# Opening attention behind the last chunk step: the last batch's ending as pieces inside attention's first steps

## The chip, the core and the metric

The kernel runs on one core of a Trainium2 chip. The metric is the device time of one launch in microseconds (us). The time before is the median of three runs; the profile is of one further execution. Five engines appear in it: TensorE (PE, with its weight loads as PEld), VectorE (DVE), ScalarE (ACT), GpSimd (POOL) and SyncE (SP, which here only issues transfers). ACT and POOL issue transfers as well.

## The reference

The program is two layers on 8 batches of 512 tokens with 256 features. The first adds a state-space block and a top-1 mixture of experts to the input; the second adds an attention block and a capacity-limited top-2 mixture.

```python
x  = u                                            # (8, 512, 256) f32
xn = layernorm(x)
x  = x + ssd_block(xn) + ffn_top1(xn)             # layer 0
xn = layernorm(x)
x  = x + attention(xn) + ffn_top2(xn)             # layer 1

def ssd_block(u):       # chunked scan of 128 tokens, forward and backward
    z, xBC, dt = split(u @ in_proj.T)
    ...
    yg = y * silu(z)                                            # "gate"
    yn = yg * rsqrt(mean(yg * yg, -1) + 1e-5) * norm_w          # "squares", "scale"
    return yn @ out_proj.T                                      # "output"

def attention(x):       # 16 heads of 16
    q = x @ Wq;  latent = (x @ Wk + x @ Wv) @ W_down
    k = latent @ W_up_k;  v = latent @ W_up_v
    s = clip(q k^T / 16) * decay(|i - j|);  a = softmax(clip(s))
    return (a @ v) @ Wo

def ffn_top2(x):        # 7 experts and one that does nothing, 512 rows of capacity each
    w = softmax(x @ router.T + b);  keep the two largest
    each expert takes the first 512 tokens that chose it, in order
    return sum of weight * relu(rows @ W1[e]) @ W2[e], and x * weight for the idle expert
```

## The kernel before

The instructions of each engine stand in the order in which the program traces them (`tc.manual_schedule`), so the order of generators and `yield`s in the source is the order on the chip. An engine's instruction waits only for semaphores of what it reads, or of what last used the place that it writes.

**Layer 0.** The scan runs in 64 chunk steps, 8 for each batch. A step issues a chunk's own work and some pieces of its neighbours (`others(n)`): the next batch's convolutions, and the past batch's ending: `gate` (reads the tokens `u` by a transfer, multiplies y by z, squares), `squares` (the matmul `ss`, L1040, and its copy), `scale` (the matmul `sm`, L1047, and a reciprocal root), and `output` (the matmul `op`, L1060, for each of four token tiles, and `xr`, L1067, the addition of the tokens). Between them `fill(k)` advances two other generators: `rows`, the layer-0 experts, and when these are at an end `rest`, which is `late()`.

**The chain `late()`.** It first loads the weights of layer 1 (`second_weights`, in which `base`, L860, is computed) and then turns three generators in rotation: `norm(b)` (layer norm of batch b, stored as `xn1`), `turn(b)` (two transposed halves `tp1`, L737; the router's `pp1`, L744, copied to `proj1` by DVE, L749; then `project`: `lp` L246 and its copy `lat`, `qp` L261 twice, `kp` L270 twice, `vp` L279 twice, each copied by ACT and stored to DRAM) and `route(lo, hi)` (which expert slots the tokens take: DVE and POOL work, the matmuls `both`, L172, and one accumulated matmul group `tab1` (L226) for each batch, built from DVE's `en_r`, `en_w` and added to `slots`, L819). `route` runs for batches 0 to 4, and then for 5 to 7, which needs `pp1` of batch 7.

**Banks.** Every one of these matmul groups takes a PSUM buffer by `bank(...)` and gives it back when ACT or DVE has copied it. In layer 0 the endings take the tag "gen" and `late()` the tag "e", each with two buffers. In attention `bank` is this:

```python
def bank(name, shape):
    return psum.tile(shape, FP, name=name, tag="bank", bufs=1)
late_bank = bank
```

so that `late()`, the experts and `finish` share one buffer there. Of the other seven, scores (`s_ps`) have four, transposes (`p_ps`) two and values (`o_ps`) one.

**The end of layer 0.** After chunk step 63 the ending of batch 7 runs as a block of its own, with `fill` between its pieces, and only then do the pools of layer 0 close and those of attention open, at the same places.

**Attention.** There are 128 steps (batch b, group g of four heads, token tile c). Step n issues the scores (L1533: four matmuls), the clamp and the banded row maximum on DVE (L1538, L1540), then for older steps the exponentials on ACT (L1548), four transposes of 128x512 (L1555) with their copies on ACT (L1556), and, every second step, the values (L1564). Between these pieces `fill()` advances one thing: `urgent` work first, the experts as far as `due()` allows, and else `late()` through `last_rows(1)`. When `late()` is at an end, the pools of its tiles close and the experts of layer 1 start (`e_tp` L1375, `e_hp` L1383, `e_yp` L1396); `due()` spreads them evenly up to step 117. `spread` (L1418) loads q and k of a batch by groups of 16 rows: 16 transfers each. For batch 0, q goes by SP and k by ACT, traced ahead of the first step. `divide`, `finish` and `combine` normalise, project and add up the results.

**Pools.** A tile's place is freed when its pool closes. What takes a place in a pool opened later waits for the old occupants of it.

Of the kernel before, what the change touches and what calls it, by code (L numbers as in the profile page):

```python
# [17 lines left out]
P = 128  # L18
# [41 lines left out]
def tile_kernel(ctx: ExitStack, tc: tile.TileContext, t, out: bass.AP):  # L60
# [237 lines left out]

    l0 = ctx.enter_context(ExitStack())
    l0c = l0.enter_context(tc.tile_pool(name="l0c", bufs=1))  # L300
    m1 = l0.enter_context(tc.tile_pool(name="m1", bufs=1))
    m2 = l0.enter_context(tc.tile_pool(name="m2", bufs=2))
    mp = l0.enter_context(tc.tile_pool(name="mp", bufs=1, space=PSUM))
    r0 = ExitStack()
    r0p = r0.enter_context(tc.tile_pool(name="r0", bufs=2))
    r0b = r0.enter_context(tc.tile_pool(name="r0b", bufs=1))
# [5 lines left out]
    def ask():  # L312
        pool, tag, bufs = ((m1, "z", 1), (m2, "yT", 2), (m2, "yT", 2), (m2, "bc", 2))[len(us)]
        both = pool.tile([P, HC, S], FP, name=tag, tag=tag, bufs=bufs).rearrange("p k s -> p (k s)")
        us.append(both.rearrange("p (t d) -> p t d", d=DM))
        for k in range(2):
            Y.dma_start(
                out=us[-1][:, k * TPB : (k + 1) * TPB, :], in_=rows_of(t["u"], order[2 * len(us) - 2 + k])
            )
# [14 lines left out]
    w_out = ctile("w_out", [P, HC, DM], pool=l0c)  # L334
# [5 lines left out]
    share = ctile("share", [P, 1], pool=l0c)  # L340
# [223 lines left out]
    with ExitStack() as es:  # L564
# [28 lines left out]
        def blocks():  # L593
            nonlocal e2
            r0.close()
            e2 = es.enter_context(tc.tile_pool(name="e2", bufs=2, side="right"))
# [74 lines left out]
        def late():  # L671
# [12 lines left out]
            def norm(b):  # L684
# [4 lines left out]
                if b == B - 1:  # L689
                    x = final  # L690
                else:
                    if b not in asked:
                        ask(b)
                        yield
                        yield
                        add(b)
                        yield
                        yield
                        yield
                    x = asked.pop(b)  # L700
                    Y.dma_start(out=rows_of(x1, b), in_=x)
# [27 lines left out]
            def turn(b):  # L729
# [18 lines left out]
                yield  # L748
# [12 lines left out]
            def route(lo, hi):  # L761
# [5 lines left out]
                with tc.tile_pool(name=f"rt{lo}", bufs=1, side="right") as pool:  # L767
# [33 lines left out]
                with tc.tile_pool(name=f"en{lo}", bufs=1, side="right") as pool:  # L801
# [31 lines left out]
        def second_weights():  # L833
# [3 lines left out]
            l1c = ctx.enter_context(tc.tile_pool(name="l1c", bufs=1, side="right"))  # L837
            tl = tls.enter_context(tc.tile_pool(name="tl", bufs=1, side="right"))
# [65 lines left out]
        class Batch:  # L904
# [68 lines left out]
            def start(self):  # L973

                self.yT = p2.tile([P, HC, S], FP, name="yT", tag="yT")

                def first(k):
                    by = V if self.b else G
                    by.tensor_tensor(self.yT[:, k, :], self.x[:, k, :], self.fr[k], ALU.mult)
                    if k + 2 < HC:  # L980
                        self.ask(k + 2)

                def second(k):
                    y, x = self.yT[:, k, :], self.x[:, k, :]
                    for to, of in ((slice(1, S), slice(0, S - 1)), (slice(0, S - 1), slice(1, S))):
                        V.scalar_tensor_tensor(y[:, to], x[:, of], d_rep[:, k : k + 1], y[:, to], ALU.mult, ALU.add)

                return chain([(p, k) for k in range(HC) for p in (first, second)])
# [25 lines left out]
            def z_part(self, o):  # L1014

                if o == 0:
                    self.z = p1.tile([P, HC, S], FP, name="z", tag="z")
# [5 lines left out]
            def gate(self):  # L1023
                self.u = p1.tile([P, TPB, DM], FP, name="u", tag="u", bufs=2)
# [32 lines left out]
            def output(self, c):  # L1057
# [6 lines left out]
                def add():  # L1064
# [3 lines left out]
                    if c == TPB - 1:  # L1068
                        Y.dma_start(out=rows_of(x1, self.b), in_=final if self.b == B - 1 else self.u)
# [125 lines left out]
        with tc.manual_schedule(engines=ENGINES):  # L1195
# [116 lines left out]
            pending.append(last.gate())  # L1312
            while pending:
                slot()
                fill(1)
            last.squares()
            fill(3)
            slot(last.scale)
            fill(3)
            slot()  # L1320
            while B - 4 not in turned:
                fill(1)
            final = tl.tile([P, TPB, DM], FP, name="xr", tag="xr", bufs=3)
            for c in range(TPB):
                slot(lambda: last.output(c))
                fill(2)
            slot()
            batch_done = B
    l0.close()
# [3 lines left out]
    res = l1.enter_context(tc.tile_pool(name="res", bufs=1))  # L1333
    x_sb = res.tile([P, NTILE, DM], FP, name="x_sb", tag="x_sb")
    with tc.tile_pool(name="a1", bufs=1) as p1, tc.tile_pool(name="a2", bufs=2) as p2, tc.tile_pool(
        name="ap", bufs=1, space=PSUM
    ) as psum, ExitStack() as es:

        def bank(name, shape):
            return psum.tile(shape, FP, name=name, tag="bank", bufs=1)  # L1340
# [69 lines left out]
        def spread(rows, got, n, by=None):  # L1410

            for g in range(4):
                wide = p2.tile([P, S], FP, name=n + "T", tag=n + "T", bufs=6)
# [16 lines left out]
        def inputs_of(b):  # L1430
            rows, vd = kept.pop(b)
            got = {"q": [], "k": [], "v": p2.tile([P, TPB, VW], FP, name="vt", tag="vt")}
# [29 lines left out]
        class Ending:  # L1462
# [22 lines left out]
            def project(self):  # L1485
# [3 lines left out]
                V.tensor_tensor(x_sb[:, self.i, :], x_sb[:, self.i, :], fp, ALU.add)  # L1489
                Y.dma_start(out=out[self.i * P : (self.i + 1) * P, :], in_=x_sb[:, self.i, :])  # L1490

        def finish(b, oT):
            for c in range(TPB):
# [3 lines left out]
                fo = p2.tile([P, DM], FP, name="fo", tag="fo")  # L1497
                A.copy(fo, fp)
                xi = x_sb[:, b * TPB + c, :]
# [4 lines left out]
        def combine():  # L1504


            def add(b):
                G.dma_start(out=x_sb[:, b * TPB : (b + 1) * TPB, :], in_=rows_of(x1, b), accum_op=ALU.add)
# [7 lines left out]
            for b in range(B - 1):  # L1516
                G.dma_start(out=rows_of(out, b), in_=x_sb[:, b * TPB : (b + 1) * TPB, :])
# [3 lines left out]
        class Step:  # L1521
# [4 lines left out]
            def scores(self):  # L1526
# [7 lines left out]
                self.p = [p2.tile([P, S], FP, name="s1", tag="s1", bufs=12) for _ in range(4)]  # L1534
                mx = p2.tile([P, 4], FP, name="mx", tag="mx", bufs=4)
                self.ng = p2.tile([P, 4], FP, name="ng", tag="ng", bufs=4)
# [13 lines left out]
            def transpose(self, pT, heads):  # L1550
                cc = self.c % 2
                for i in heads:
                    pp = psum.tile([P, TPB, P], FP, name="p_ps", tag="p_ps", bufs=2)
# [16 lines left out]
        def divide(b, g, op, od, rd, held):  # L1570


            if b == B - 1:
                if g == 0:
                    held.append(p1.tile([P, KC, S], FP, name="oT", tag="oT"))
# [12 lines left out]
            if j == 0:  # L1588
                held.append(p1.tile([P, KC, S], FP, name="oT", tag="oT"))
# [20 lines left out]
        with tc.manual_schedule(engines=ENGINES):  # L1610
            rows, vd = kept.pop(0)
            got = {"q": [], "k": [], "v": p2.tile([P, TPB, VW], FP, name="vt", tag="vt")}
            spread(rows["q"], got["q"], "q", Y)
            spread(rows["k"], got["k"], "k", A)
# [17 lines left out]
            def last_rows(k):  # L1632

                nonlocal late_left
                for _ in range(k):
                    if next(rest, "end") == "end":
                        late_left = False
# [22 lines left out]
            def follow():  # L1660
# [4 lines left out]
                elif ready is None:  # L1665
                    ready = n
                    tls.close()
                    e1 = es.enter_context(tc.tile_pool(name="f1", bufs=1, side="right"))
                    e2 = es.enter_context(tc.tile_pool(name="f2", bufs=2, side="right"))
# [5 lines left out]
            def own_rows(b):  # L1675
                Y.dma_start(out=x_sb[:, b * TPB : (b + 1) * TPB, :], in_=rows_of(xn1, b))
# [6 lines left out]
            for n in range(N + 3):  # L1683

                if n < N:
# [7 lines left out]
                    if b == B - 1 and g == 0:  # L1693
                        xi = x_sb[:, b * TPB + c, :]
# [19 lines left out]
                begun = n >= 1  # L1714
                m = n - 2
                pair = m >= 2 and m % 2 == 0
                if pair:

                    s = done[m - 1]
                    if s.c == 1:  # L1720
                        s_op = psum.tile([P, S], FP, name="o_ps", tag="o_ps", bufs=1)
# [8 lines left out]
                if 0 <= m < N:  # L1730
                    if m % 2 == 0:
                        s_pT = [p2.tile([P, TPB, 2 * P], FP, name="pT", tag="pT", bufs=5) for _ in range(4)]
# [108 lines left out]
```

## Time and profile before

| | |
|---|---|
| median of three runs | 2022.19 us (2018.9, 2033.09, 2022.19) |
| the profiled execution | 2011.26 us |
| its span | 2009.5 us |
| PE busy | 1818.5 us, 90% |
| DVE busy | 1459.0 us, 73% |
| ACT busy | 1176.2 us, 59% |
| POOL busy | 587.2 us, 29% |
| mean granted TensorE clock | 0.943 |

The page gives the busy time of each engine, and the span cut into 40 slices of 50.2 us, each with a digit for the busy tenths. "PEclk" is the clock that TensorE was granted, as a share of full speed. In lists of instructions, `out<-in` names the tiles by the program's names, an L number is a line of the kernel, and square brackets hold the idle time before a group with what ended it. Times within the span count from its start. The profiled execution is 10.9 us shorter than the median of the runs.

### The profile page before, as it was taken

Reading aid. Unit: us, or ns where it says so; the run is one execution under the profiler, and the core shown is the slowest. Engines: PE = TensorE matmul, PEld = TensorE weight load, DVE = VectorE, ACT = ScalarE, POOL = GpSimd, SP = SyncE. Lnnn points to the kernel's source line nnn. Section 1 sums busy time; section 2 is a strip of 40 time slices with the busy share of each in tenths; the row PEclk is TensorE's granted clock in tenths of the full one; section 3 lists DMA queues with packets and bytes.
Section 4 is the critical chain, followed back from the end, with each engine's and each line's share of the span. In section 5 each row is a group of like instructions: output and inputs, shape, how many; then the busy total and the mean of one; then the engine's idle time right before and its main releaser. Section 6 shows DMA issues by size and latency. Waiting matters only on the chain.

```text
span 2009.5 us, 33675 instructions
## 1 busy us (share of the span) xinstructions
PE 1818.5 (90%) x11956; PEld 1239.9 (62%) x11956; DVE 1459.0 (73%) x3344; ACT 1176.2 (59%) x2575; POOL 587.2 (29%) x528
## 2 busy tenths in 40 slices
PE   6566999899999999998898869999999999999997
PEld 6224677676767767664565546666666666666654
DVE  6587675767667576778557477878888878788885
ACT  4232454434545454454552337878887887788886
POOL 0042665655556574543330000101011111111030
PEclk8677999999999999998898679999999999999999
DMA  7010565545556554436553313222313222223171
GB/s 267 6 47 26 211 212 171 180 143 172 197 171 206 170 189 160 161 104 172 154 165 93 98 44 108 66 84 57 89 49 103 66 85 54 87 57 100 40 143 42
DMA packets 132967, 238.58 MB, mean 119 GB/s; under 512 B 20381, under 2 KB 94111, under 8 KB 120896
## 3 DMA queue, kind: packets, MB, share of 16 engines
q1 hardware_dynamic: 101952, 119.99, 19.1%
q0 software_dynamic: 29808, 115.78, 18.7%
q8 instruction: 96, 1.57, 0.3%
q10 hardware_dynamic: 1040, 0.66, 0.1%
q14 instruction: 71, 0.58, 0.1%
HBM read 183.58 MB, written 53.71 MB: 118 GB/s over the span
## 4 chain that ended last, share of the span: by engine, by line
PE 66%; DVE 14%; ACT 11%; issue 2%; DMA 1%; POOL 0%; SPq 0%; ACTq 0%; DVEq 0%; POOLq 0%
PE p_ps L1555 8%; PE h_ps L634 6%; PE pj L915 6%; PE y_ps L655 6%; ACT s L1548 6%; PE o_ps L1564 6%; PE s_ps L1533 4%; PE e_hp L1383 4%; PE e_yp L1396 4%; ACT pT L1556 3%; PE op L1060 3%; PE yd L1141 3%; PE seg L1103 2%; PE sp L1171 2%; PE yoff L1159 2%
## 5 line engine op out<-in xcount | busy, mean ns | idle before, releaser
L1538 DVE TENSOR_SCALAR s<-s_ps 128x512 f32<-128x512 f32 x512 | 318.0, 684 | 137.2 <-PE s_ps L1533 135.5
L1548 ACT ACTIVATE s<-s,ng 128x512 f32<-128x512 f32 x512 | 330.9, 717 | 10.9 <-DVE ng L1544 10.9
L1540 DVE CUSTOM_DVE_ANT_0 s<-s,band 128x512 f32<-128x512 f32 x512 | 323.1, 689 | 0.0
L1556 ACT COPY pT<-p_ps 128x512 f32<-128x512 f32 x512 | 276.0, 588 | 65.1 <-PE p_ps L1555 57.1
L1555 PE MATMUL p_ps<-ident,s 128*128 128x128 f32 x2048 | 285.7, 283 | 21.1 <-ACT pT L1556 15.0
L1555 PEld LDWEIGHTS p_ps<-ident,s 128*128 128x128 f32 x2048 | 236.1, 144 | 95.5 <-ACT pT L1556 31.7
L1403 POOL DMA_INDIRECT x<-e_yo,number x28 | 45.9, 1639 | 626.8 <-ACT e_yo L1402 620.8
L915 PE MATMUL pj<-xT,w_w_in 128*128 128x512 f32 x384 | 201.1, 650 | 12.7 <-DVE cv L928 6.6
L634 PEld LDWEIGHTS h_ps<-xdT,w 128*128 128x128 f32 x1248 | 151.7, 195 | 20.6 <-issue 19.8
L1533 PE MATMUL s_ps<-kT,qT 16*128 16x512 f32 x1024 | 157.4, 659 | 5.3 <-DMA kT<-kd 2.2
L928 DVE SCALAR_TENSOR_TENSOR cv<-pj,w_conv_w,cv 128x511 f32<-128x511 f32 (+2 forms) x192 | 143.3, 747 | 22.7 <-ACT cv L924 18.2
L634 PE MATMUL h_ps<-xdT,w 128*128 128x128 f32 x1248 | 155.0, 279 | 0.1
L655 PE MATMUL y_ps<-w,hT 128*128 128x256 f32 x624 | 147.7, 380 | 0.0
L1087 POOL TENSOR_TENSOR au<-da,half 128x512 f32<-128x512 f32 x64 | 78.4, 1225 | 202.8 <-PE seg L1103 131.7
L655 PEld LDWEIGHTS y_ps<-w,hT 128*128 128x128 f32 x624 | 115.7, 190 | 32.4 <-issue 17.1
L1383 PE MATMUL e_hp<-e_xdT,e_w 128*128 128x256 f32 x448 | 121.5, 394 | 10.9 <-ACT e_hT L1386 8.8
L915 PEld LDWEIGHTS pj<-xT,w_w_in 128*128 128x128 f32 x384 | 71.1, 203 | 96.0 <-issue 81.1
L1564 PE MATMUL o_ps<-pT,vt 128*32 128x256 f32 x2048 | 126.8, 386 | 0.0
L1150 DVE TENSOR_TENSOR yT<-yT,yd 128x512 f32<-128x512 f32 (+1 forms) x64 | 43.8, 684 | 98.8 <-PE yd L1141 98.3
L1396 PE MATMUL e_yp<-e_w,e_hT 128*128 128x256 f32 x448 | 113.3, 385 | 0.2 <-ACT e_hT L1386 0.2
L1564 PEld LDWEIGHTS o_ps<-pT,vt 128*32 128x32 f32 x2048 | 61.1, 111 | 83.0 <-issue 49.6
L1116 ACT ACTIVATE mt<-seg,mid 64x64 f32<-64x64 f32 x512 | 109.4, 309 | 0.7
(326 smaller groups left out, 3033.4 us busy)
## 6 DMA issues: line engine op xcount, KB each, us to landing
ex<-exd SPq DMA_DIRECT2D x96, 128.0 KB
fr<-fdd SPq DMA_DIRECT2D x64, 128.0 KB
od<-os SPq DMA_DIRECT2D x28, 256.0 KB
e_w<-in_ei_dram SPq DMA_DIRECT2D x7, 1024.0 KB
e_w<-in_eo_dram SPq DMA_DIRECT2D x7, 1024.0 KB
vd<-vt SPq DMA_DIRECT2D x16, 288.0 KB
vt<-vd SPq DMA_DIRECT2D x8, 576.0 KB
u<-in_u_dram SPq DMA_DIRECT2D x8, 512.0 KB
```

The lines of the kernel that those rows point to most:

```text
L634: T.matmul(hp[:, i, :], w1[:, k * FF + f * P : k * FF + (f + 1) * P], xdT[:, k * P : (k + 1) * P], start=(k == 0), stop=(k == KC - 1),)
L655: T.matmul(yp, hT[f // 4][:, f % 4, :], w2[:, f * DM : (f + 1) * DM], start=(f == 0), stop=(f == FC - 1))
L915: T.matmul(pj, w_in[:, k, o * P : (o + 1) * P], self.xT[:, k, :], start=(k == 0), stop=(k == KC - 1))
L1383: T.matmul(hp, w1[:, k, f * P : (f + 1) * P], xdT[:, k, :], start=(k == 0), stop=(k == KC - 1))
L1396: T.matmul(yp, hT[:, f, c * P : (c + 1) * P], w2[:, f, :], start=(f == 0), stop=(f == FC - 1))
L1533: T.matmul(sp[i], self.q[r, cols], self.k[r, :], start=True, stop=True)
L1538: V.tensor_scalar(self.p[i], sp[i], -CLAMP, CLAMP, ALU.max, ALU.min)
L1540: V.tensor_tensor_reduce(out=self.p[i], in0=self.p[i], in1=band[:, at : at + S], scale=1.0, scalar=-3.0e38, op0=ALU.mult, op1=ALU.max, acc ...
L1548: A.activation(self.p[i], self.p[i], AF.Exp, bias=self.ng[:, i : i + 1])
L1555: T.transpose(pp[:, k, :], self.p[i][:, k * P : (k + 1) * P], ident)
L1556: A.copy(pT[i][:, :, cc * P : (cc + 1) * P], pp)
L1564: T.matmul(op[32 * i : 32 * i + 32, half * 2 * P : (half + 1) * 2 * P], self.v[:, k, h * (AD + 1) : h * (AD + 1) + 32], pT[i][:, k, :], st ...
```

## The change

It has three parts, and the order of the instructions up to chunk step 63 is the same.

First, the block after chunk step 63 becomes a generator `ending()`. Only work that is already pending is drained before the pools close. `last_rows(1)`, called by `fill()` in attention, now advances `end_chain` and `rest` by one piece each, and `fill()` works from step 0 on (`begun = True`) where it worked from step 1 on.

Second, tiles that the ending needs (`z`, odd batches' `yT` and `u`, `w_out`, `share`) lie in a pool `mz` that stays open into attention. The sums `x_sb` are cut into four pieces, two of which take the places of `yT` and `z` in `mz` later, and `oT` takes that of `u`. Attention's one two-buffer pool and its PSUM pool are cut into several pools by tag, with the same numbers of buffers except `fo`, which has six where it had two.

Third, nearly all pools are opened with `reuse_waits="tile"`: a tile at a used place waits for the tiles that lay there, where it waited before for all that the older pool held there.

Besides, the store of `x1` for the last batch is issued by `norm`, k is loaded ahead of q for batch 0, and `turn` has one `yield` fewer in the last two batches.

```diff
+    mz = ctx.enter_context(tc.tile_pool(name="mz", bufs=1, reuse_waits="tile"))
     l0 = ctx.enter_context(ExitStack())
-    l0c = l0.enter_context(tc.tile_pool(name="l0c", bufs=1))
+    l0c = l0.enter_context(tc.tile_pool(name="l0c", bufs=1, reuse_waits="tile"))
...
-    w_out = ctile("w_out", [P, HC, DM], pool=l0c)
+    w_out = ctile("w_out", [P, HC, DM], pool=mz)
...
                     x = asked.pop(b)
-                    Y.dma_start(out=rows_of(x1, b), in_=x)
+                Y.dma_start(out=rows_of(x1, b), in_=x)
...
-                yield
+                if b < B - 2:
+                    yield
                 V.tensor_copy(proj1[:, b * TPB : (b + 1) * TPB, :], pp)
...
-                self.yT = p2.tile([P, HC, S], FP, name="yT", tag="yT")
+                pool, tag = (mz, "yTz") if self.b % 2 else (p2, "yT")
+                self.yT = pool.tile([P, HC, S], FP, name="yT", tag=tag, bufs=1)
...
-                self.u = p1.tile([P, TPB, DM], FP, name="u", tag="u", bufs=2)
+                pool, tag = (mz, "uz") if self.b % 2 else (p1, "u")
+                self.u = pool.tile([P, TPB, DM], FP, name="u", tag=tag)
...
-                    if c == TPB - 1:
-                        Y.dma_start(out=rows_of(x1, self.b), in_=final if self.b == B - 1 else self.u)
+                    if c == TPB - 1 and self.b < B - 1:
+                        Y.dma_start(out=rows_of(x1, self.b), in_=self.u)
...
             last = batch[B - 1]
-            pending.append(last.gate())
             while pending:
                 slot()
-                fill(1)
+            gated = last.gate()
+
+        def ending():
+            nonlocal gated, final, batch_done
+            while callable(gated):
+                gated = gated()
+                yield
+            yield
             last.squares()
-            fill(3)
-            slot(last.scale)
-            fill(3)
-            slot()
+            yield
+            last.scale()()
+            yield
             while B - 4 not in turned:
-                fill(1)
+                yield
             final = tl.tile([P, TPB, DM], FP, name="xr", tag="xr", bufs=3)
             for c in range(TPB):
-                slot(lambda: last.output(c))
-                fill(2)
-            slot()
+                last.output(c)()
+                yield
             batch_done = B
+
+        end_chain = ending()
     l0.close()
...
-    x_sb = res.tile([P, NTILE, DM], FP, name="x_sb", tag="x_sb")
-    with tc.tile_pool(name="a1", bufs=1) as p1, tc.tile_pool(name="a2", bufs=2) as p2, tc.tile_pool(
-        name="ap", bufs=1, space=PSUM
-    ) as psum, ExitStack() as es:
+    sums = {}
+
+    def x_of(b):
+        two = b // 2
+        if two not in sums:
+            pool, tag = (res, "x0") if two == 0 else (res, "x1") if two == 1 else (mz, "yTz") if two == 2 else (mz, "z")
+            both = pool.tile([P, HC, S], FP, name="x_sb", tag=tag, bufs=1).rearrange("p k s -> p (k s)")
+            sums[two] = both.rearrange("p (t d) -> p t d", d=DM)
+        return sums[two][:, b % 2 * TPB : (b % 2 + 1) * TPB, :]
+
+    with ExitStack() as es:
+
+        def pool(name, bufs=1, **kw):
+            return es.enter_context(tc.tile_pool(name=name, bufs=bufs, reuse_waits="tile", **kw))
+
+        p1, pk, p2, pq = pool("a1"), pool("ak"), pool("a2", 2), pool("aq")
+        few, turns, psum = pool("ab", space=PSUM), pool("at", space=PSUM), pool("ap", space=PSUM)
 
         def bank(name, shape):
-            return psum.tile(shape, FP, name=name, tag="bank", bufs=1)
+            return few.tile(shape, FP, name=name, tag="bank", bufs=1)
...
-                fo = p2.tile([P, DM], FP, name="fo", tag="fo")
+                fo = p2.tile([P, DM], FP, name="fo", tag="fo", bufs=6)
...
+            spread(rows["k"], got["k"], "k", A)
             spread(rows["q"], got["q"], "q", Y)
-            spread(rows["k"], got["k"], "k", A)
...
                 for _ in range(k):
-                    if next(rest, "end") == "end":
-                        late_left = False
+                    late_left = [next(one, "end") for one in (end_chain, rest)] != ["end", "end"]
...
-                begun = n >= 1
+                begun = True
```

## The prediction

> **What bounds the kernel now.** First the page's forty slices (50.2 us each), for where TensorE is idle or slow. PE is busy for nine tenths through most of the second half, but in slices 22 and 23 (1105 to 1206 us) the digits fall to 8 and 6, and the granted clock to 0.6 and 0.7. That is where attention opens, and where the diff works.
>
> ```profile
> PE   6566999899999999998898869999999999999997
> ...
> PEclk8677999999999999998898679999999999999999
> ```
>
> Then the busy times of four stretches, cut where the work changes: from the scores of the last chunk step to the first scores of attention (1128.70), to the first transpose of batch 7 (1146.60, "point A"), to the first expert transpose (1224.60), and on to 1900. The columns are PE, PE weight loads, DVE, ACT, POOL, then PE's granted clock and the DMA share. The fifth row is a part of the first stretch.
>
> ```profile
> 1074.00:1128.70 54.70, 48.52 (x241) 35.30 (x239) 27.10 (x87) 13.19 (x24) 1.43 (x2) 0.81 0.23 66
> 1128.70:1146.60 17.90, 13.07 (x33) 6.03 (x33) 12.92 (x41) 1.99 (x4) 0.00 (x0) 0.50 0.48 148
> 1146.60:1224.60 78.00, 57.95 (x364) 37.74 (x364) 54.08 (x170) 38.69 (x69) 4.38 (x5) 0.74 0.24 77
> 1224.60:1900.00 675.40, 645.41 (x5181) 437.50 (x5178) 552.80 (x1410) 555.50 (x1036) 70.28 (x50) 1.00 0.26 72
> 1098.00:1112.00 14.00, 13.33 (x47) 11.09 (x47) 3.99 (x19) 2.34 (x4) 0.00 (x0) 0.51 0.12 43
> ```
>
> Once the experts run, PE is busy 645.41 of 675.40 us (96%): it is the bound. In the 150.6 us before that it is busy 48.52 + 13.07 + 57.95 = 119.5 us, 79%, and DVE 94.1. So some 31 us of PE idleness lie there, partly at half clock. The chain of waits says why attention opens at 1128.7: the last addition of `output` releases the loads of kT and qT, because the new pools lie where the old ones were.
>
> ```profile
> 1125.44 0.49 DVE xr L1067
> 1125.94 0.02 issue
> 1125.96 2.33 DMA kT<-kd
> 1128.29 0.02 issue
> 1128.31 4.03 DMA qT<-qd
> ```
>
> The PE timeline gives the pace of the `bank` fills on either side.
>
> ```profile
> 1077.33 1.72 PE L246 MATMUL lp<-xT,w_kv 128*64 128x256 f32 x8
> 1081.12 3.63 PE L261 MATMUL qp<-xT,w_w_q 128*128 128x512 f32 x4 [2.07 <-DVE proj L749]
> ...
> 1100.74 3.66 PE L226 MATMUL tab<-en_w,en_r 128*128 128x56 f32 x16 [0.67 <-ACT vt L280]
> ...
> 1125.33 1.14 PE L279 MATMUL vp<-w_uv,lat 64*128 64x256 f32 x8
> ...
> 1146.60 1.95 PE L737 MATMUL tp<-ident,xr 128*128 128x128 f32 x4 [1.77 <-ACT xr L721]
> ...
> 1161.75 1.97 PE L246 MATMUL lp<-xT,w_kv 128*64 128x256 f32 x8 [5.44 <-DVE proj L749]
> ...
> 1171.14 1.13 PE L270 MATMUL kp<-lat,w_uk 64*128 64x256 f32 x4 [0.69 <-ACT qc L263]
> ...
> 1179.29 1.13 PE L279 MATMUL vp<-w_uv,lat 64*128 64x256 f32 x4
> ```
>
> From the `lp` at 1077.33 to the end of the last `vp` at 1126.47 there are 28 fills of a bank (lp, qp, tab, qp, tab, ss, and so on). There are two tags of two buffers each, so a fill need not wait for the evacuation of the one just before it: 49.1 / 28 = 1.75 us a fill. From 1146.60 to 1180.42, inside attention, the same kinds of fill (two tp, pp, lp, two qp, two kp, two vp) have one buffer: 33.8 / 10 = 3.4 us a fill. The idle of 5.44 us before `lp` is a fill waiting until DVE, busy with a step's rows, copies `proj`.
>
> **The change, part by part.** (1) Attention opens behind chunk step 63. Its loads no longer wait for the place (pools reuse by tile, some tiles live in `mz`). In the compiled order of the changed kernel the first scores stand right behind `pp` of batch 6, so they start near 1080 and not at 1128.7. The 28 fills then follow on the one `bank`, between steps 0 to 3. Nothing of their work is removed: gate, squares, scale, four outputs, batch 6's projections, the five table passes all stay.
>
> (2) What it brings: at the transpose of batch 7 (call it point B) attention has issued the scores of steps 0 to 4, against 0 to 2 at A. From B to the first expert transpose the order is that of before: seven steps lie between, 78 us. So two steps are done earlier and need not be done at the end. A step's PE work is taken from the groups:
>
> ```profile
> L1538 DVE TENSOR_SCALAR s<-s_ps 128x512 f32<-128x512 f32 x512 | 318.0, 684 | 137.2 <-PE s_ps L1533 135.5
> ...
> L1540 DVE CUSTOM_DVE_ANT_0 s<-s,band 128x512 f32<-128x512 f32 x512 | 323.1, 689 | 0.0
> ...
> L1555 PE MATMUL p_ps<-ident,s 128*128 128x128 f32 x2048 | 285.7, 283 | 21.1 <-ACT pT L1556 15.0
> ...
> L1533 PE MATMUL s_ps<-kT,qT 16*128 16x512 f32 x1024 | 157.4, 659 | 5.3 <-DMA kT<-kd 2.2
> ...
> L1564 PE MATMUL o_ps<-pT,vt 128*32 128x256 f32 x2048 | 126.8, 386 | 0.0
> ```
>
> (285.7 + 157.4 + 126.8) / 128 = 4.45 us on PE, and (318.0 + 323.1) / 128 = 5.0 us on DVE. PE bounds the later stretch, so two steps are worth 2 × 4.45 / 0.956 = 9.3 us. The ends are nothing (if the cover only moves idle time) and 13.0 us (two steps at their own pace with experts between them: 77 steps from 1300 to 1800 us, 6.49 us each). I take 9.3.
>
> (3) What it costs: B against A. `lp` in the new order waits for `proj`, which stands on DVE behind the eight row operations of step 0. `pp` ends at 1077.4; scores at half clock 2.3 us (the four at 1128.70), DVE 5.0, the copies round them 1.3 (an estimate from the 0.6 us rows of ACT and DVE): `lp` at about 1086, 9 us later than now. Then 28 fills: at 1.75 us each B is 1086 + 49 = 1135; at 3.4 us each it is 1086 + 95 = 1181. My walk through the order with every wait named (`tab` waits for ACT's `qc`; `qp` and `kp` wait for DVE's `slots`, itself behind `en_r`, `en_w` and the rows of a step) gives 1165 if all matmuls run at the full-clock durations of before, and 1198 if all run at half clock (a `tab` 3.66 us instead of 1.96, a `qp` 3.63 instead of 1.96). I take 1181: the fills are of the same kinds, have the same single buffer and the same step work between them as the ten that were measured, and it lies between the walks. B − A = +34.6 us; by the walks +18.4 and +51.4.
>
> [...]
>
> On the clock, the row from 1098 to 1112 shows 0.51 with PE busy for 13.33 of 14.00 us. [...]
>
> (4) Queues. The sixteen kT issues go to ACT's queue at about 1076, ahead of the gate's squares and of `lat`; from 1125.96 to 1137.45 they took 11.5 us now, 0.72 us each. `lat` is wanted about 1088, when they are through: 0 us, covered by step 0's DVE work and the wait for `proj`; without that cover up to 11.5 us, and `kp` would be late next, with PE waiting for it. The sixteen qT issues go to SP behind the load of `u` (10.9 us); behind them wait vt, `w_o` and later vd stores, none wanted before the first `o_ps`: 0 to 4 us (qT's landing at 1128.31 took 4.03), I take 0. The `x1` store of batch 7 moves from the output to `norm`, one issue of 0.43 us each way: 0. The swap of k before q and two fewer idle turns: 0, within a fill (3.4 at most either way).
>
> (5) Waits by tile elsewhere. At 878.9 DVE stands 2.58 us because `base` takes a place whose pool waits for a DMA. In the new order that wait is gone, and so are some on POOL and SP. Between 0 (other work hides it) and 2.6 us; I take 2, since DVE's row work follows at once. Deeper `fo` buffers: 0, `finish` is 28 pieces spread over the stretch where PE is 96% busy.
>
> **Sum.** +34.6 − 9.3 − 2 = +23 us on the profiled execution's 2011.26: 2034 (its span of 2009.5 becomes 2033). The median shown is 2022.19, 10.9 above that execution, so I carry the difference to it: 2045. The ends of this mechanism: +18.4 − 13.0 − 2.6 = +3 (2025) and +51.4 − 9.3 − 2 = +40 (2062).
>
> **Rivals.** *Faster: the one bank doesn't bind.* While a fill waits, PE now has transposes and scores of a step to do, which it lacked before. If each fill turns round in the 1.75 us of the two-tag stage, B is 1135, 11.6 us ahead of A, and the sum −11.6 − 9.3 − 2 = −23: 1999. For it: PE idles 31 us of 150 there, which steps could fill. Against it: the 3.4 us were measured with steps between the fills. It decides from B = 1157.9 on, that is 2.57 us a fill.
>
> *About no change: the clock stays full.* Step work in the gaps keeps PE busy, B is the 1165 of the full-clock walk, and the sum +18.4 − 9.3 − 2 = +7: 2029. For it: 0.81 in the first stretch, where PE was 89% busy. Against it: 0.50 and 0.74 once attention runs with one buffer.
>
> *Half clock throughout.* +40: 2062. For it the 0.50 from 1128.70 to 1146.60, in which two or three steps and no experts run, as they would from 1080 on; against it 0.74 from 1146.60.
>
> *The change doesn't do what it says.* If the first loads still wait for a place or a DMA until 1126, the scores stand at 1128.7 as now, and the 28 fills behind them: all of the forecast 48.7 us later, +72, 2094. In the compiled order the first kT load waits for one POOL operation of the last chunk and older DMAs only.
>
> **How the numbers follow.** Chances: forecast 0.45, full clock 0.22, half clock 0.15, faster 0.15, not as said 0.03. A measurement of this kernel can tell about 1% from no change: 2002 to 2042. The forecast's own range is 2030 to 2062, and a third of it lies below 2042; with the full-clock case that makes 0.15 + 0.20 + 0.02 of others for the same, 0.16 for faster, 0.47 for slower. The range 2008 to 2068 leaves out most of the faster case and a little at the top.
>
> **What would show it.** Right: first `s_ps` near 1080, `tp` of batch 7 near 1181, the first expert transpose near 1259 behind scores of step 11, a granted clock of 0.5 to 0.8 between, PE waits before fills released by ACT `qc`, `kc`, `vt` and DVE `proj`, `slots`, and from 1259 on the stretch to the end shorter by 9 us. Wrong: `tp` of batch 7 before 1158, or fills that no longer wait for an evacuation, or first scores still near 1128.

## The result and the profile after

The changed kernel takes 2030.41 us (median of 20 runs, 2026.55 to 2040.45) against 2016.80 us (20 runs, 2009.38 to 2033.09): a ratio of 1.0064, 95% interval 1.0047 to 1.0081, so it is slower by 13 us (13.6 between the medians). The profiled execution after took 2028.93 us, its span is 2027.2 us. The forecast was 2045, slower, by 23 us.

The slices of the page after, with 50.7 us each: the dip is longer. The four slices 21 to 24 (1064 to 1267 us) have the digits 6, 7, 7 and 8 and a clock of 0.6, 0.6, 0.8 and 0.7, where before slices 21 to 23 had 8, 8 and 6.

```profile
PE   6557999998999999998896778999999999999997
...
PEclk8678999999999999998896687999999999999999
```

The busy times of stretches after, cut at the same events as before: batch 5's transposes to the first late fill `lp`, on to batch 7's transposes, on to the first expert transpose, and on. Columns: PE, PE weight loads, DVE, ACT, POOL, granted clock, DMA share, GB/s.

```profile
1069.40:1084.49 15.09, 5.24 (x34) 3.60 (x32) 12.62 (x48) 2.41 (x5) 1.44 (x2) 0.69 0.65 141
1084.49:1179.48 94.99, 75.23 (x313) 48.29 (x313) 41.02 (x121) 24.76 (x44) 0.00 (x0) 0.68 0.18 60
1179.48:1252.29 72.81, 57.61 (x377) 37.93 (x373) 51.83 (x167) 36.01 (x65) 4.43 (x5) 0.78 0.21 70
1252.29:1900.00 647.71, 621.40 (x4979) 422.73 (x4976) 527.69 (x1342) 531.21 (x992) 71.29 (x50) 1.00 0.27 75
```

The same events in the PE timeline before: batch 5's transposes, the first scores of attention, the first expert transpose (batch 7's transposes, at 1146.60, stand in the prediction).

```profile
1073.60 1.34 PE L737 MATMUL tp<-ident,xr 128*128 128x128 f32 x8
...
1128.70 2.27 PE L1533 MATMUL s_ps<-kT,qT 16*128 16x512 f32 x4 [2.22 <-DMA kT<-kd]
...
1224.64 0.66 PE L1375 MATMUL e_tp<-ident,e_xd 128*128 128x128 f32 x4
```

The PE timeline after shows the mechanism row by row: the first scores at 1073.61 and not at 1128.70, then `lp` held back behind step 0's rows on DVE, then a fill, a wait for its copy, and the next fill.

```profile
1069.38 1.04 PE L738 MATMUL tp<-ident,xr 128*128 128x128 f32 x8
...
1073.61 2.10 PE L1560 MATMUL s_ps<-kT,qT 16*128 16x512 f32 x8 [0.69 <-DMA kT<-kd]
1084.49 1.97 PE L246 MATMUL lp<-xT,w_kv 128*64 128x256 f32 x8 [8.77 <-DVE proj L751]
...
1097.84 3.66 PE L226 MATMUL tab<-en_w,en_r 128*128 128x56 f32 x16 [0.74 <-ACT qc L263]
1103.12 2.04 PE L270 MATMUL kp<-lat,w_uk 64*128 64x256 f32 x4 [1.61 <-DVE slots L821]
1105.89 3.66 PE L226 MATMUL tab<-en_w,en_r 128*128 128x56 f32 x16 [0.73 <-ACT kc L272]
...
1179.48 1.12 PE L738 MATMUL tp<-ident,xr 128*128 128x128 f32 x4
...
1185.19 1.08 PE L246 MATMUL lp<-xT,w_kv 128*64 128x256 f32 x8 [0.28 <-DVE proj L751]
...
1252.29 0.66 PE L1401 MATMUL e_tp<-ident,e_xd 128*128 128x128 f32 x4
```

And on DVE, between step 0's clamp and the copy of `proj` that `lp` waits for:

```profile
1078.52 2.48 DVE L1565 TENSOR_SCALAR s<-s_ps 128x512 f32<-128x512 f32 x4
...
1084.16 0.18 DVE L751 COPY proj<-pp 128x32 f32<-128x32 f32 x1
```

From `lp` to batch 7's transposes 28 fills took 94.99 us: 3.39 us each. Within them PE stood 95.0 − 75.2 = 20 us, and worked at a mean clock of 0.68. (The `pp` that the prediction calls batch 6's is batch 5's; batch 6's is one of the 28 fills. Nothing in the sum hangs on it.)

Cut at the same three events, batch 5's transposes (T5), batch 7's (T7) and the first expert transpose, the two profiled executions differ like this:

| stretch, us | before | after | difference | predicted |
|---|---|---|---|---|
| start to T5 | 1073.60 | 1069.38 | −4.2 | −2 |
| T5 to T7 | 73.00 | 110.10 | +37.1 | +34.6 |
| T7 to experts | 78.04 | 72.81 | −5.2 | 0 |
| experts to the end | 784.86 | 774.91 | −10.0 | −9.3 |
| span | 2009.5 | 2027.2 | +17.7 | +23 |

The profiled execution of before lies 5.5 us below the median of its 20 runs and that after 1.5 below, which is the 4 us between +17.7 here and +13.6 in the medians. The −4.2 up to T5 lies within the scatter of T5 (below).

### The profile page after: what moved, and what is told of

Read it like the earlier page. It is cut to its first block, busy times and chain, and to the rows that moved or that the text cites. A ratio compares the mean times of both kernels' runs of the same rounds, so it can differ in the third digit from the quotient of the medians.

```text
span 2027.2 us, 33672 instructions
## 1 busy us (share of the span) xinstructions
PE 1824.0 (90%) x11956; PEld 1239.6 (61%) x11956; DVE 1460.0 (72%) x3344; ACT 1175.8 (58%) x2575; POOL 591.7 (29%) x528
## 4 chain that ended last, share of the span: by engine, by line
PE 69%; DVE 15%; ACT 11%; issue 3%; DMA 1%; POOL 0%; SPq 0%; ACTq 0%; DVEq 0%; POOLq 0%
PE p_ps L1582 8%; PE pj L917 7%; PE h_ps L635 6%; PE y_ps L656 6%; PE o_ps L1591 6%; ACT s L1575 5%; PE s_ps L1560 4%; PE e_hp L1409 4%; PE e_yp L1422 4%; ACT pT L1583 3%; PE op L1064 3%; PE yd L1145 3%; PE seg L1107 2%; DVE cv L930 2%; PE sp L1175 2%
## 5 line engine op out<-in xcount | busy, mean ns | idle before, releaser
L1560 PE MATMUL s_ps<-kT,qT 16*128 16x512 f32 x1024 | 151.9, 654 | 0.7 <-DMA kT<-kd 0.7
```

The lines of the kernel that those rows point to most:

```text
L1560: T.matmul(sp[i], self.q[r, cols], self.k[r, :], start=True, stop=True)
```

## The experiments

Theory: the fills are dear since each waits for the copy of the one before it in the single `bank`. Rivals: the half clock would cost the same with any number of buffers; the steps' rows on DVE hold the copies back; the pools and places cost the time. All ratios are against the kernel before, run on the same chip.

The events of each profile, in us:

| kernel | T5 | first scores | T5 to T7 | T7 to experts | experts to end | ratio, 95% interval |
|---|---|---|---|---|---|---|
| before | 1073.6 | 1128.7 | 73.0 | 78.0 | 784.9 | 1 |
| after | 1069.4 | 1073.6 | 110.1 | 72.8 | 774.9 | 1.0064 (1.0047 to 1.0081) |
| two places | 1078.3 | 1081.8 | 78.5 | 74.3 | 772.2 | 0.9918 (0.9897 to 0.9939) |
| four places | 1067.7 | 1071.1 | 82.6 | 73.9 | 772.2 | 0.9884 (0.9860 to 0.9909) |
| four, and scores' place later | 1071.0 | 1074.5 | 78.2 | 68.8 | 772.1 | 0.9884 (0.9858 to 0.9911) |
| four, one piece ahead | 1068.7 | 1077.6 | 76.0 | 81.3 | 772.5 | 0.9912 (0.9879 to 0.9945) |
| after, one piece ahead | 1070.1 | 1081.8 | 114.6 | 81.4 | 772.3 | 1.0104 (1.0075 to 1.0132) |
| after, yield put back | 1072.1 | 1075.9 | 110.6 | 78.5 | 772.4 | 1.0095 (1.0070 to 1.0120) |
| after, ending as a block | 1075.5 | 1134.2 | 74.3 | 76.5 | 789.3 | 0.9976 (0.9956 to 0.9996) |
| after, a quarter of the table pass | 1074.4 | 1077.9 | 102.0 | 66.4 | 773.7 | one run |
| before, one buffer each | 1074.3 | 1153.9 | 97.9 | 83.5 | 784.8 | 1.0113 (1.0085 to 1.0140) |
| before, two buffers shared | 1078.1 | 1139.9 | 79.8 | 80.6 | 784.9 | 1.0010 (0.9991 to 1.0028) |
| before, waits by tile | 1078.3 | 1136.0 | 76.2 | 84.5 | 784.9 | 1.0009 (0.9986 to 1.0032) |

T5 itself scatters from 1068 to 1078 us over kernels of the same order up to there, so a single profile tells the whole time to some 5 us only; the stretches after T5 and the ratios are used below. These stretches scatter too: the two kernels "four places" and "four, and scores' place later" have the same order up to T7, and took 82.6 and 78.2 us from T5 to T7.

**Two places for the fills.**

```diff
+        at_step, spare = 0, itertools.cycle(range(2))
         def bank(name, shape):
+            if at_step < 4 and next(spare):
+                return few.tile(shape, FP, name=name, tag="o_ps", bufs=1)
             return few.tile(shape, FP, name=name, tag="bank", bufs=1)
...
             for n in range(N + 3):
+                at_step = n
```

> The changed kernel, but until step 4 the fills of the late chain and of the ending alternate between the bank and the place of o_ps, which no value uses before step 4. One-buffer theory (a fill waits for the copy of the one before: 28 fills in 95.0 us, 3.39 us each, between the first lp at 1084.49 and the transpose of batch 7 at 1179.48): fills at 2.0 to 2.5 us, the transpose of batch 7 at 1140 to 1155, the whole 25 to 35 us shorter than the changed kernel, about 2000 us, ratio to before 0.990 to 0.995. Clock theory (PE is busy 75.2 of the 95 us because its granted clock is 0.68, and would stay busy): only the 20 us without PE work can go, and the half clock stays: at best 1160, ratio 0.998 to 1.003. Row theory (DVE's rows of the steps hold the copies back): no change of more than 5 us, ratio 1.004 to 1.007.

2000.71 us, ratio 0.9918, T5 to T7 31.6 us shorter than in the changed kernel. The one-buffer theory holds and the other two fall at this point. The PE timeline of this kernel has the same fills in the same order, now mostly back to back:

```profile
1110.78 3.66 PE L226 MATMUL tab<-en_w,en_r 128*128 128x56 f32 x16
1114.23 1.82 PE L1051 MATMUL sm<-share,ssr 128*128 128x1 f32 x8
1116.05 2.04 PE L279 MATMUL vp<-w_uv,lat 64*128 64x256 f32 x4
1118.02 3.66 PE L226 MATMUL tab<-en_w,en_r 128*128 128x56 f32 x16
1121.47 3.74 PE L1064 MATMUL op<-w_out,yT 128*128 128x256 f32 x8
...
1156.84 0.66 PE L738 MATMUL tp<-ident,xr 128*128 128x128 f32 x4
```

No bracket stands behind these rows: nothing waited. The 31.6 us split into three: `lp` comes 6.6 us after T5 where it came 15.1 (−8.5); from there to T7 PE stands 9.8 us where it stood 19.8 (−10); and its busy time falls from 75.2 to 62.1 us (−13) for the same instructions, at a granted clock of 0.76 and not 0.68:

```profile
1084.90:1156.84 71.94, 62.11 (x313) 41.83 (x312) 47.30 (x141) 23.96 (x44) 0.00 (x0) 0.76 0.25 77
```

The rows of DVE still count for something: of the 9.8 us, 5.45 stand before the first `qp`, which now waits for `proj` where `lp` did. That the clock rose because the waits went isn't shown. Two profiles of kernels further below, with four places, leave it open: PE stands still less in them, 6.9 and 7.7 us from `lp` to T7, yet the clock is no higher, 0.71 and 0.76 in the same order of work, and their busy times differ by 5.3 us. (The second row is the kernel with the scores' place later.)

```profile
1074.59:1150.28 75.69, 68.75 (x312) 47.23 (x313) 47.36 (x140) 23.96 (x44) 0.00 (x0) 0.71 0.23 72
1077.98:1149.16 71.18, 63.44 (x312) 43.74 (x312) 46.85 (x140) 24.07 (x44) 0.00 (x0) 0.76 0.24 77
```

**Four places in the first two steps.**

```diff
+            k = next(spare)                       # cycle(range(4))
+            if at_step < 2 and k % 2:
+                return turns.tile(shape, FP, name=name, tag="p_ps", bufs=2)
+            if at_step < 4 and (k == 2 if at_step < 2 else k % 2):
+                return few.tile(shape, FP, name=name, tag="o_ps", bufs=1)
```

> As with two places, but in steps 0 and 1 the fills rotate through four places (bank, o_ps and both of p_ps, which no transpose uses before step 2), as many as in the kernel before. One-buffer theory: a few us shorter than with two places, 0 to 5, since two already separate a fill from the copy before it; ratio to before 0.988 to 0.995. Clock theory: the same as with two places, 0.998 to 1.003. Row theory: no change, 1.004 to 1.007.

1994.92 us, ratio 0.9884: it beats both kernels, by 35 us and 22 us. Against two places the intervals overlap, and T5 to T7 is no shorter in the profiles (82.6 and 78.2 against 78.5), so two places are enough for the main effect.

**The ending as a block again**, the rest of the change kept: the diff's removed lines behind `last = batch[B - 1]` put back, and `end_chain = iter(())`.

> The changed kernel with the move alone undone: the ending runs as a block ahead of attention again, in the two-buffer tags, in the order of before; the pool that outlives layer 0, the waits by tile and the early loads stay. If the move into one buffer is the whole loss: the 110.1 us between the transposes of batch 5 and of batch 7 go back to 66 to 73, ratio to before 0.993 to 0.999. It also tells whether the new places make layer 0 shorter: six runs of the changed kind reached batch 5's transposes at 1068 to 1078 us, mean 1071, three of the kind before at 1074 to 1078, mean 1075. If so, that point lies at 1071 or earlier here; if that is only spread, the ratio is 0.996 to 1.000. Rival, that pools or places cost the time: ratio 1.004 or more.

2013.91 us, ratio 0.9976. T5 to T7 is back at 74.3 us. The move alone therefore costs 1.0064 / 0.9976 = 1.0088, some 18 us (13 to 23 by the two intervals), and the remainder of the change gains about 5 (1 to 9). T5 at 1075.5 gives no sign that the new places shorten layer 0, though one profile can't tell that from the scatter.

**Fewer buffers in the kernel before.** Two edits; the first replaces each allocation from the ending on by two of a two-buffer tag, the second gives each chain one tile that is written again and again.

```diff
 # two buffers shared
+        if closing:
+            mp.tile(shape, FP, name=name + "_off", tag="e", bufs=2)
+            return mp.tile(shape, FP, name=name, tag="e", bufs=2)
 # one buffer each
+        if closing is not None:
+            flat = closing[tag == "e"][: shape[0], : ...]
+            ...
+            closing = [mp.tile([P, S], FP, name="closing", tag=tag, bufs=2) for tag in ("gen", "e")]
```

> The kernel before, with its order untouched, but from the end of chunk step 63 to the opening of attention each fill takes the same one buffer (every second allocation of a two-buffer tag is left unused). One-buffer theory: the fills from the first gate on, 1.75 us each before, take 2.6 to 3.2 us even without attention steps between them, so the first scores come 20 to 35 us later; ratio 1.010 to 1.017. Clock theory: PE is at half clock there anyway (0.51 from 1098 to 1112 us), so at most 8 us more, ratio up to 1.004.

2020.67 us, ratio 1.0010: far from 20 to 35 us. The edit did not do what that text says. In its timeline fills follow each other without waiting for the copy just before (`qp` at 1092.79 right behind `tab` at 1090.55, with no wait), so the unused allocations seem to have held no place, and the fills to have alternated between two buffers that both chains shared, where there had been four. What it shows is that two shared ones are nearly enough: 6.8 us from T5 to T7, and no difference in the ratio.

> The kernel before, order untouched, but from the end of chunk step 63 to the opening of attention the late chain has one buffer and the ending one, where each has two. One-buffer theory (waiting for the copy is itself the cost, with or without attention steps between): each of the 21 late fills waits 0.7 to 1.2 us more, 15 to 25 us from the transposes of batch 5 to the first scores (55.1 us before), ratio 1.007 to 1.012. Rival, that one buffer is dear only because DVE's and ACT's work of the steps stands between a fill and its copy: at most 7 us, ratio up to 1.004.

2041.56 us, ratio 1.0113: T5 to the first scores took 79.6 us and not 55.1, +24.5, as the one-buffer theory said, without one attention step between the fills. Of these, 14.3 us are PE standing (20.4 against 6.2) and 10.3 a longer busy time, at a clock of 0.72 against 0.80 from `lp` to the first scores. (That a copy can find the next fill's numbers in place of its own in this kernel, and that tokens are then routed otherwise, is the author's reading, which no run shows; the instructions are the same.) Its timeline has the pattern of the changed kernel:

```profile
1101.79 3.67 PE L226 MATMUL closing<-en_w,en_r 128*128 128x56 f32 x16 [0.68 <-ACT kc L272]
1106.97 2.07 PE L270 MATMUL closing<-lat,w_uk 64*128 64x256 f32 x4 [1.52 <-DVE slots L827]
1109.72 3.66 PE L226 MATMUL closing<-en_w,en_r 128*128 128x56 f32 x16 [0.68 <-ACT kc L272]
```

**Waits by tile alone**: `reuse_waits="tile"` on all SBUF and PSUM pools of the kernel before.

> The kernel before with reuse_waits by tile on all SBUF and PSUM pools, and nothing else of the change: every engine's order is that of before. By the prediction's fifth part the wait of base goes (2.6 us or less), and kT and qT can be loaded before the last output (2.22 us of PE idle before the first scores, 1.42 before the next): 2 to 6 us shorter, ratio 0.997 to 0.999. Rival, that the waits by tile themselves cost the 13 us of the change: ratio 1.004 or more.

2018.83 us, ratio 1.0009, interval 0.9986 to 1.0032. The rival falls; a gain of up to 3 us isn't excluded and none is shown.

**A piece of the late chain ahead of step 0**, in the changed kernel and in that with four places: `last_rows(2)` for `last_rows(1)` ahead of the steps.

> The changed kernel, with one more piece of the late chain traced ahead of step 0, so that the copy of proj and the fill lp stand before the first scores on DVE and PE. If the 8.77 us that PE stood before lp are a term of its own (the copy behind step 0's rows): 5 to 9 us shorter than the changed kernel, ratio to before 1.002 to 1.004. If the one buffer sets the pace whatever comes first: within 2 us of it, 1.005 to 1.007.

2040.46 us, ratio 1.0104: some 8 us slower, which neither theory expected. The wait moved:

```profile
1079.88 1.98 PE L246 MATMUL lp<-xT,w_kv 128*64 128x256 f32 x8 [6.24 <-DVE proj L751]
...
1128.92 2.07 PE L279 MATMUL vp<-w_uv,lat 64*128 64x256 f32 x4 [3.47 <-DVE ms L1056]
```

`lp` still waits 6.24 us: the routing's short operations on DVE (`so_sk`, `lc_i`, `place`) and two rows of `z` and `yT` stand ahead of `proj` in either order, and only step 0's rows, which came on top, are gone. Since all later pieces moved against the steps, `ms` now stands behind a step's rows, where `vp` waited 0.25 us in the changed kernel. T7 also comes one step earlier in the order (ahead of step 4's scores), so more steps remain: T7 to the experts is 81.4 us.

> The kernel with four places in steps 0 and 1 and the same one piece ahead of step 0. PE stood 3.57 us for en_w there, which was queued behind step 0's rows on DVE. That wait goes: 2 to 5 us shorter than with four places alone, ratio to before 0.986 to 0.988. If DVE or the half clock sets the pace: no change, 0.988.

2000.51 us, ratio 0.9912, slower than four places alone if anything. T5 to T7 is 6.6 us shorter (2.2 against the other profile with four places), T7 to the experts 7.4 us longer, for the same reason. What is drawn ahead at one end is missing at the other.

**A second place after step 4**: with four places before it, `late()`'s fills then alternate between `bank` and the scores' four buffers until the experts start.

```diff
+            if at_step >= 4 and k % 2 and ready is None:
+                return psum.tile(shape, FP, name=name, tag="s_ps", bufs=4)
```

> The kernel with four places, and from step 4 until the experts start the late fills alternate between the bank and the scores' four buffers. From batch 7's transposes to the first expert transpose it took 73.9 us, with 8.97 us of waiting for en_w and about 6 us of waits for a copy (0.28, 0.47, 0.72, 0.68, 1.61 and others). One-buffer theory: those 6 us go, ratio to before 0.985 to 0.987. Rival: the table's DVE work sets the end of that stretch and scores lose a buffer, so no gain or a loss, 0.988 to 0.992.

T7 to the experts is 68.8 us, 5.1 less, as the theory said; the ratio is 0.9884, the same as without it (1995.98 us). At five and six runs 5 us can't be told by the ratio, so the gain is seen in one profile only (three others with one bank behind T7 took 72.8, 73.9 and 74.3).

**A quarter of the table pass**, in the changed kernel.

```diff
-                                enter(tp, ready[h], h == 0, h == 1)
+                                enter(tp, [one[:, :1] for one in ready[h]], h == 0, h == 1)
```

> The changed kernel with six of the eight matmuls of each expert table's pass over a batch left out (most tokens get no expert slot in layer 1); every fill, wait and copy stays. Between the transposes of batch 5 and 7 five of these passes of 3.66 us lie on the path. Waiting theory: only their own time goes, 5 x 3.66 x 0.75 = 13.7 us of 110.1, granted clock still about 0.68. Clock theory, that these small matmuls keep the clock at half and so double everything else: the clock rises to 0.9 or more and 30 to 40 us go.

T5 to T7 takes 102.0 us, 8.1 less, and the other fills run no faster: a `qp` takes 3.65 us, against 1.96 at a clock of 1.00 (before, at 1168.49), and from `lp` to T7 the clock is 0.70 (0.68 with the whole pass).

```profile
1095.89 0.65 PE L226 MATMUL tab<-en_w,en_r 128*128 128x56 f32 x4 [0.74 <-ACT qc L263]
1099.14 3.65 PE L261 MATMUL qp<-xT,w_w_q 128*128 128x512 f32 x4 [2.60 <-DVE slots L821]
```

The clock theory in this form falls. The five passes took 16.6 us in the changed kernel (one ran at 1.99 us) and 4.6 here, so 12.0 us of their own time went, and some 4 came back, in part as longer waits: 2.60 us for `slots` where it was 1.6 to 1.9, because DVE builds the next entries ahead of that addition (in the changed kernel 0.69, 0.27 and 0.39 us for `en_r`, `en_b` and `en_w` before `slots` at 1094.16).

**The dropped yield put back**, in the changed kernel.

```diff
-                if b < B - 2:
-                    yield
+                yield
```

> The changed kernel with the one dropped yield of turn put back for the last two batches, so that a piece of attention's work again stands between the router's matmuls and the copy of proj on DVE. The prediction priced this edit at nothing. From batch 7's transposes to the first expert transpose the changed kernel took 72.8 us and the kernel before 78.0; in that stretch lp waited 0.28 us for proj against 5.44. If the dropped yield is what saved there: 77 to 79 us again, lp waits 4 us or more, ratio to before 1.008 to 1.010. If the saving comes from the steps that were done earlier: 72 to 74 us, ratio 1.005 to 1.007.

2034.34 us, ratio 1.0095. T7 to the experts is 78.5 us again, and the wait is there:

```profile
1187.82 2.09 PE L1559 MATMUL s_ps<-kT,qT 16*128 16x512 f32 x8
1195.37 1.97 PE L246 MATMUL lp<-xT,w_kv 128*64 128x256 f32 x8 [5.46 <-DVE proj L750]
```

The scores of a step are traced between `pp` and the copy of `proj`; so a copy of 0.18 us on DVE comes behind 5 us of rows, and `lp` behind it. Without the `yield` the copy stands ahead of them and `lp` waited 0.28 us. The row settles where the time goes; the ratio alone would not, since its interval overlaps that of the changed kernel.

## Why the prediction was right in kind and off in size

The direction and the mechanism held. Attention did open at 1073.6 ("near 1080"), the transposes of batch 7 came at 1179.48 ("near 1181"), the fills waited for `qc`, `kc`, `vt`, `proj` and `slots` as named, and the clock lay at 0.68 in that stretch. The two walks, 1165 and 1198, enclosed it.

That the times agree so closely is partly luck. `lp` at 1084.49 was put at 1086, but T5 came 4.2 us earlier than before, and `lp` 15.1 us after T5 where the sum has 12.4. A fill took 3.39 us against the 3.4 taken from ten fills of the kernel before, but not for the same reasons. In those ten, 33.8 us hold 11.4 us of the steps' own matmuls, 14.4 of the fills' and 8.1 without PE work; in the 28 fills, 95.0 us hold 15.1, 60.1 and 19.8. A fill's own matmuls rose from 1.4 to 2.1 us (`tab` at 3.66 us and `op` at 3.75 are not among the ten, and the clock was 0.76 there), the step work for each fill fell from 1.1 to 0.5. "The same kinds" and "the same step work" did not hold, and the two errors cancelled.

The step that failed is the last item of the fourth part, "the swap of k before q and two fewer idle turns: 0". One of those turns is the `yield` between the router's matmuls and `proj`. The prediction itself showed the 5.44 us before `lp` and named DVE's rows as their cause, but it did not ask what in the diff would take that wait away. Put back, it costs 5.7 us from T7 to the experts, and 0.3% in the ratio. With it the forecast's +23 compares with the 1.0095 of that kernel, +19 us. The assumption "from B to the first expert transpose the order is that of before: 78 us" was wrong by the same 5.2 us.

A second term was too small. The two earlier steps, put at 9.3 us, are worth 10.0 from the first expert transpose to the end in the profile after, but 11.2 to 12.8 in the seven other profiles in which the experts start behind step 11 (772.1 to 773.7 against 784.9). That is near the upper end of 13.0, two steps at their own pace.

The rest of the 10 us between +23 and +13.6 is mainly the choice of one execution each: the pair of profiles differs by 17.7 us, the medians by 13.6. The profile before was a short one: from T7 to the experts it took 78.0 us, where three other profiles with that order took 80.6, 83.5 and 84.5. The median of three runs shown, 2022.19, lies 5.4 above that of twenty, which moved the forecast's 2045 but not its difference.

The 2 us for waits by tile are not shown by any run. The costs put at 0 for ACT's kT issues and for SP's queue hold: the first `qp` waited 0.46 us for `lat`, and the first values (`o_ps`, 1175.91) waited for nothing. The 10.9 us that the prediction sets beside the load of `u` are shown by no row; SP's sixteen qT issues ran from 1126.00 to 1137.81 in the kernel before, two stores among them.

The rivals. "Faster, the one bank doesn't bind" did not come about in the change itself, and its turning point was wrong. By the prediction's sum, 2.57 us a fill means no change. With two places a fill takes just that (71.94 / 28), T7 comes 78.5 us after T5, and yet the kernel is 0.8% faster than before, some 16 us. The yield makes about 5 of them, the two steps 3 more (12.7 and not 9.3), and `lp`, which comes 6.6 us after T5 and not 12.4, another 6. "The clock stays full" did not come about, and "half clock throughout" was nearly so for half of the stretch: from 1084 to 1140 the clock is 0.56, and from the scores at 1143.56 on (1.14 us, where they took 2.09 at 1109.48) most rows run as long as those of the kernel before at a clock of 1.00 (`kp` 1.13 us in both); up to T7 the clock is 0.88.

What a place is worth, the runs show: one more takes 31.6 us off T5 to T7 here, one buffer for each chain in place of two adds 24.9 in the kernel before (97.9 against 73.0), and for a third and fourth place nothing certain is shown.

## What to carry over

When work is moved between two stages, move its buffers too: count the places that a stage holds idle at that time (here `o_ps` until step 4 and `p_ps` until step 2) and let the moved work rotate through them; one such place was worth 31.6 us here. Ask of every small copy what is traced ahead of it on its engine; a copy of 0.18 us behind a step's rows held TensorE for 5.44 us in the kernel before and for 5.46 with the `yield` put back. And a piece drawn ahead at one end of a fixed order changes which copy stands behind which rows all along it (some 8 us slower in the changed kernel), so it is judged over the whole transition.

## What was not expected of the hardware

The half clock outlasted 39 us of unbroken work. The rival "the clock stays full" counted on step work that keeps PE busy; but in the profile of the kernel with four places PE is busy for 39.09 of 39.10 us (the profile models where matmuls end) and granted 0.54:

```profile
1082.80:1121.90 39.10, 39.09 (x140) 29.32 (x141) 20.73 (x60) 6.38 (x11) 0.00 (x0) 0.54 0.15 54
```

The half clock is not a property of this order of work. In the profile of the kernel with the scores' place later, whose order is the same up to T7, some 10 us of unbroken work at 0.55 were followed by 9 us at 1.00:

```profile
1086.22:1095.80 9.58, 9.58 (x36) 7.47 (x36) 5.76 (x14) 2.34 (x4) 0.00 (x0) 0.55 0.27 103
1095.80:1105.00 9.20, 9.20 (x66) 6.72 (x66) 8.73 (x24) 1.76 (x3) 0.00 (x0) 1.00 0.18 60
```

Leaving out three quarters of the small table matmuls in the changed kernel hardly raised the clock (0.70 against 0.68 from `lp` to T7). What ends the half clock in this stretch stays open.
